# Own scores stored in one transfer, a weight load moved up, and a table tile read in six transfers by ScalarE's queue

## The chip, the cores and the metric

The kernel runs on one core of a Trainium2 chip. Its metric is the device time of one execution in microseconds (us). The engines are PE (TensorE, matrix products), DVE (VectorE), ACT (ScalarE), POOL (GpSimd) and SP (SyncE). Each has an instruction queue of its own that runs in order; they wait for each other by semaphores. ACT, POOL and SP also issue transfers (DMAs), which run beside the engines on 16 DMA engines. In the profile, q0 is POOL's queue of transfers, q1 SP's and q10 ACT's.

## The reference

The kernel computes two layers of a graph network on 625 nodes with 1024 features and 10000 edges. The changed part lies in the first layer, which adds to x a graph attention over the edges, a linear attention over all nodes and, after them, a small ternary feed-forward net. The graph attention is the part that matters here:

```python
xl = (x @ Wl).reshape(n, H, D)          # H = 4 heads of D = 64
xr = (x @ Wr).reshape(n, H, D)
msg = xl[src] + xr[dst]                 # per edge, and per node with itself
act = jnp.where(msg > 0, msg, NEG_SLOPE * msg)
e = jnp.einsum('ehd,hd->eh', act, att)
m = jax.ops.segment_max(e, dst, num_segments=n)
p = jnp.exp(e - m[dst])
denom = jax.ops.segment_sum(p, dst, num_segments=n)
alpha = p / (denom[dst] + 1e-16)
out = jax.ops.segment_sum(alpha[..., None] * xl[src], dst, num_segments=n)
```

An edge from each node to itself is added to the 10000. The linear attention computes keys, values and queries with 1024x1024 weights: `kv = sum over nodes of phi(k) v`, and the answer is `phi(q) kv / (phi(q) . sum phi(k))`, with `phi(x) = elu(x) + 1`. The second layer has a mean over neighbours in place of the graph attention, and a mixture of eight experts at its end; it takes most of the time and isn't touched.

## The kernel before, in words

The nodes are worked in NT = 5 tiles of P = 125. The edges are worked in 79 chunks of 128, two chunks to a group, 40 groups. The order of the work on each engine is the order in which the program records it; nothing reorders it afterwards.

**Scores of the edges.** Tile by tile PE makes xl and xr (`left_right`, `plr`), ACT copies them into `xlr` and stores xl to DRAM as `xl_d`, POOL stores xr as `xr_d`. A "beat" (`one_beat`) handles one group. POOL gathers, for each chunk, the rows of the source nodes (`ga`, from xl_d) and of the target nodes (`gb`, from xr_d), both at L601. DVE adds and scores them four and more beats later (`score_group`, L609 and after), ACT takes the exponential (`raise_all`, `es`, L588), and POOL scatters the four scores of each edge into `table`, a 625 by 625 table of four scores in DRAM (`scatter`, L619). POOL's order within a beat is gather, scatter, gather, scatter, ... All writes of the table are ordered: a scatter waits until the write of the table before it has landed. The table was filled with zeros by SP at the start (L395). So POOL's queue holds 79 gathers of each sort and 79 scatters.

**Own scores.** In beats 5 to 9 `self_loops(t)` scores each node of tile t with itself (`own`), and ACT stores these four scores onto the table's diagonal by `rows_dma` (L654), which makes two transfers, one of 112 rows and one of 13. These stores are writes of the table too: ACT waits for the scatter before them to land, and the next scatter on POOL waits for them.

**What runs beside it.** The linear attention is worked in two halves c of 512 features. `lin.half(1)` issues the second half's loads on SP: the biases `bk_t` and `bv_t`, then Wk and Wv, each as two transfers of 1 MB (`Half`). They use a ring of six weight buffers (`wpool`). The first half's Wk and Wv are loaded at the start, with `wd` and `wlr` in the other two buffers. `work(us)` is called as PE's work is recorded, and places the beats between its pieces. The calls of `lin.key(t)` and `lin.value(t)` for each tile are in the loops over c and t at L697 and after. Behind them come queries, answers and the output product (`mixed`, L733), during which the remaining beats run with shorter lags.

**From the table to the sums.** When the last scatter is issued, `load_table(t)` brings the table's rows of tile t into SBUF as `tb` (125 partitions, five slices of 125 by 4), by two transfers of 1093.8 and 127.0 KB on POOL's queue. `weigh(t)` multiplies them by the numbers of edges `CT`, in five DVE instructions, one for each slice (L828, `pT`); `sums(t)` lets PE add them up (`pg`); `turn_sums` and `up_again` bring the result into x. The order of POOL's transfers is tb(0), x(0), tb(1), x(1) to x(4), where x(t) is the tile of the input that the layer adds to (L1021). Further tiles of the table follow later.

Of the kernel before, what the change touches and what calls it, by code (L numbers as in the profile page):

```python
# [20 lines left out]
NT = 5  # L21
P = 125
# [20 lines left out]
def gps_kernel(tc: tile.TileContext, w: dict, out: bass.AP):  # L43

    again = attempt(tc, w, out, False)
    with tc.If(again > 0):
        attempt(tc, w, out, True)  # L50
# [3 lines left out]
def attempt(ctx: ExitStack, tc: tile.TileContext, w: dict, out: bass.AP, shifted: bool):  # L54

    nc = tc.nc
# [85 lines left out]
    def nodes(t):  # L142
        return slice(t * P, (t + 1) * P)
# [18 lines left out]
    def rows_dma(eng, dst, src):  # L162

        eng.dma_start(out=dst[0:112], in_=src[0:112])
        eng.dma_start(out=dst[112:P], in_=src[112:P])
# [32 lines left out]
    wpool = graph.enter_context(tc.tile_pool(name="w", bufs=6))  # L198
# [9 lines left out]
    hold = {}  # L208

    def mid(shape, name):  # L210
        return midp.tile(shape, FP, tag="mid", name=name)
# [135 lines left out]
    with ExitStack() as st0:  # L347
# [5 lines left out]
        tview = table[0:N * N, :].rearrange("(u p d) h -> p u (d h)", u=NT, p=P)  # L353
        xnT = bigT("xnT")

        with ExitStack() as edges:
# [22 lines left out]
            def load_edges():  # L379
                for dst, name in ((si, "src"), (di, "dst")):  # L380
# [10 lines left out]
            lin = LinearAttention(xnT, ("L0_Wq", "L0_Wk", "L0_bk", "L0_Wv", "L0_bv"), w["L0_bq"],  # L391
                                  lambda us: work(us), nc.sync)
# [3 lines left out]
                              in_=none.unsqueeze(1).to_broadcast([128, 28, 440]))  # L396
# [177 lines left out]
            def score(dst, m, n, p):  # L574

                by_att = att[0:p].unsqueeze(1).to_broadcast([p, n, 256])
                if shifted:
                    nc.vector.scalar_tensor_tensor(m, m, 0.2, m, op0=ALU.mult, op1=ALU.max)
                    nc.vector.tensor_tensor(m, m, by_att, op=ALU.mult)
                else:  # L580
                    nc.vector.scalar_tensor_tensor(m, m, 0.0, by_att, op0=ALU.max, op1=ALU.mult)
                nc.vector.tensor_reduce(dst, m.rearrange("p t (h e) -> p t h e", h=4), AX.X, ALU.add)
                if not shifted:
                    nc.vector.tensor_scalar(dst, dst, LIMIT, None, op0=ALU.min)

            def exp(e):
                if not shifted:
                    nc.scalar.activation(e, e, AF.Exp)  # L588
# [35 lines left out]
            own = pool.tile([P, NT, 4], FP, name="own")  # L624
# [8 lines left out]
            diagonal = table[0:N * (N + 1), :].rearrange("(s d) h -> s d h", d=N + 1)[:, 0, :]  # L633

            def self_loops(t):


                m = pool.tile([P, 1, 256], FP, tag="xd", name="gs", bufs=1)
                nc.vector.tensor_tensor(m[:, 0, :], xlr[:, t, 0:256], xlr[:, t, 256:512], op=ALU.add)
                score(own[:, t:t + 1, :], m, 1, P)  # L640
                exp(own[:, t:t + 1, :])
                rows = xlr[:, t, 0:256].rearrange("p (h e) -> p h e", h=4)
                if shifted:
                    nc.vector.tensor_copy(xl1[:, t, :, 0:64], rows)
                else:
                    nc.vector.tensor_tensor(m[:, 0, :], xlr[:, t, 0:256], att[:P], op=ALU.mult)
                    nc.vector.tensor_reduce(linear[:, t, :], m.rearrange("p t (h e) -> p (t h) e", h=4), AX.X, ALU.add)
                    part4 = pool.tile([P, 4, 1], FP, tag="part4", name="part4", bufs=2)
                    nc.vector.tensor_scalar(part4[:, :, 0], linear[:, t, :], -4.0 * LINEAR, 4.0 * LINEAR,
                                            op0=ALU.max, op1=ALU.min)  # L650
                    nc.scalar.activation(xl1[:, t, :, 64:65], part4, AF.Exp, scale=0.25)
                    nc.vector.tensor_tensor(xl1[:, t, :, 0:64], rows,
                                            xl1[:, t, :, 64:65].to_broadcast([P, 4, 64]), op=ALU.mult)
                rows_dma(nc.scalar, diagonal[nodes(t), :], own[:, t, :])  # L654

# [14 lines left out]
            def one_beat():  # L672
                g = beat["g"]
                beat["g"] += 1
                if 5 <= g < NT + 5:
                    self_loops(g - 5)
                if lags[1] > lags[0]:
                    raise_all(g - lags[1])
                    scores(g - lags[0])
                else:  # L680
                    scores(g - lags[0])
                    raise_all(g - lags[1])
                for j in range(G):
                    if g < len(groups):
                        gather(g, j, 0)
                        scatter(g - lags[2] - 1)
                        gather(g, j, 1)
                    scatter(g - lags[2])

            def work(us):  # L690
                beat["us"] += us

                while beat["us"] >= 2.0 + 5.2 * min(beat["g"], 6) + 8.1 * max(beat["g"] - 6, 0) and chunks:
                    one_beat()
# [2 lines left out]
            states = []  # L697
            for c in range(2):
                if c:
                    lin.half(c)  # L700
                for t in range(NT):
                    for f in (lin.key, lin.value):
                        f(t)
                        part["held"] = max(part["held"] - 1, 0)
                        for _ in range(6):
                            if count():
                                work(0.7)
                states.append(lin.states())
                if c == 0:
                    for f in states[0]:  # L710
                        f()
# [63 lines left out]
            for m in range(KC):  # L775
# [5 lines left out]
                if m < 3:  # L781
# [3 lines left out]
                                      in_=w[("w_gate", "w_up", "w_down")[m]].rearrange("(k p) n -> p k n", p=128))  # L785
# [28 lines left out]
        def load_table(t):  # L814

            hold["tb", t] = mid([P, NT, P, 4], "tb")
            if not shifted:
                rows_dma(nc.gpsimd, hold["tb", t].rearrange("p s d h -> p s (d h)"),
                         tview[:, :, t * 4 * P:(t + 1) * 4 * P])

        def weigh(t):

# [194 lines left out]


        load_table(0)
        for t in range(NT):  # L1020
            rows_dma(nc.gpsimd, x[:, t, :], xrows[t])  # L1021
            if t == 0:
                load_table(1)
# [9 lines left out]
        for p in range(NT + 2):  # L1033
# [29 lines left out]
            if p + 2 < NT:  # L1063
                load_table(p + 2)
# [187 lines left out]
    for b in range(NB_MIN, NB):  # L1252
        nc.gpsimd.dma_start(out=y_d[b * 128:(b + 1) * 128, :].rearrange("p (a n) -> p a n", a=4),
                            in_=zero.unsqueeze(1).to_broadcast([128, 4, 256]))
# [452 lines left out]
    for i in range(3):  # L1707
        d = 1 << i
# [240 lines left out]
```

## Time and profile before

| | us |
|---|---|
| median of 4 runs | 2201.38 |
| the four runs | 2202.71, 2202.16, 2194.34, 2200.61 |
| the profiled execution | 2203.11 |
| its span | 2201.3 |
| PE busy | 2110.1 (96%) |
| DVE, POOL, ACT busy | 712.4, 340.3, 194.0 |
| first gather on POOL | 57.72 |
| last scatter on POOL | 413.77 |
| end of the weighing of tile 0 | 429.46 |
| mean clock of PE, share of full speed | 0.980 |

In the rows of a timeline, the first number is the start in us from the start of the span, the second the time busy; then come the engine ("ACTq" and the like for the issue of a transfer by that engine), the line, the operation, the tiles (out<-in) with the number of instructions put together, and in square brackets how long the engine had been idle and what ended the wait. A row of waits gives the engine and tile that waited, what it waited for, the us in total, the number of times and the longest. A row of a window gives the stretch and, for PE, PE's weight loads, DVE, ACT and POOL, the time busy and the number of instructions; then PE's granted clock, the share of the DMA engines that was busy and GB/s. "PEclk" in the page has a digit for each fortieth of the span, in tenths of full speed, 9 for 90% or more.

### The profile page before, as it was taken

To read this page: it belongs to the slowest core of one execution; us is meant where nothing else is said; L and a number is where in the kernel's file an instruction comes from. 1 tells how busy PE (TensorE), PEld (TensorE's weight loads), DVE (VectorE), ACT (ScalarE), POOL (GpSimd) and SP (SyncE) were. 2 spreads that over 40 slices of the span, in tenths; PEclk is the share of its full clock that TensorE was granted. 3 is DMA by queue.
4 is the path that set the end of the run, shared out by engine and by line. 5 is a ranking of instruction groups with operands and counts; after the bars stand their busy time and mean duration, and the time that the engine had idled before them with its cause. 6 is when DMAs were issued, how large, how long until landed. Compare 5 with 4: busy or idle time off the path is not lost. (4 is left out here: it accounts for less than half of the span.)

```text
span 2201.3 us, 17365 instructions
## 1 busy us (share of the span) xinstructions
PE 2110.1 (96%) x6934; PEld 1211.7 (55%) x6934; DVE 712.4 (32%) x1214; ACT 194.0 (9%) x354; POOL 340.3 (15%) x349
## 2 busy tenths in 40 slices
PE   7999999589899999999999999999999999999998
PEld 6665564355455777754446777457744444444443
DVE  5786486467432740000122143322111111111012
ACT  2010110002201100000000111100000000000000
POOL 1676767400000200210000000110000000000011
PEclk9999999679999999999999999999999999999999
DMA  9235432440122110150303101022099988997732
GB/s 301 80 94 187 136 120 87 100 127 22 38 86 77 48 39 16 71 182 0 96 19 106 51 26 39 29 95 96 25 363 343 330 294 306 331 330 284 276 140 91
DMA packets 145848, 301.62 MB, mean 137 GB/s; under 512 B 12370, under 2 KB 22436, under 8 KB 145754
## 3 DMA queue, kind: packets, MB, share of 16 engines
q1 hardware_dynamic: 123700, 244.23, 31.2%
q0 software_dynamic: 17376, 46.42, 7.1%
q10 hardware_dynamic: 4678, 9.72, 1.4%
q8 instruction: 58, 0.95, 0.2%
q14 instruction: 36, 0.29, 0.0%
HBM read 277.49 MB, written 22.84 MB: 136 GB/s over the span
## 5 line engine op out<-in xcount | busy, mean ns | idle before, releaser
L130 PE MATMUL pu<-w,xgT 128*128 128x512 f32 x768 | 333.9, 593 | 1.9 <-DVE xgT L1243 1.9
L130 PEld LDWEIGHTS pu<-w,xgT 128*128 128x128 f32 x768 | 144.3, 190 | 174.6 <-issue 171.7
L130 PE MATMUL pyb<-w,hb 128*128 128x512 f32 x384 | 174.3, 599 | 2.4 <-ACT yb L105 2.1
L130 PE MATMUL pk<-w,xnT 128*125 128x512 f32 x320 | 141.4, 595 | 1.2 <-DMA w<-in_L_Wk_dram 1.0
L130 PE MATMUL pv<-w,xnT 128*125 128x512 f32 x320 | 141.8, 597 | 0.2
L130 PE MATMUL pq<-xnT,w 128*128 128x313 f32 x512 | 138.2, 429 | 1.0 <-DVE v L277 0.8
L130 PE MATMUL p<-tT,w 128*128 128x313 f32 x512 | 136.3, 428 | 0.4 <-DVE tT L1243 0.4
L130 PEld LDWEIGHTS pyb<-w,hb 128*128 128x128 f32 x384 | 70.0, 190 | 90.8 <-issue 74.7
L130 PEld LDWEIGHTS pq<-xnT,w 128*128 128x128 f32 x512 | 97.5, 191 | 40.0 <-DVE v L277 1.6
L1783 DVE TENSOR_TENSOR su<-pu,su 128x512 f32<-128x512 f32 x24 | 16.6, 691 | 314.6 <-ACT su L1782 314.6
L130 PEld LDWEIGHTS p<-tT,w 128*128 128x128 f32 x512 | 97.0, 190 | 37.7 <-issue 1.2
L130 PEld LDWEIGHTS pv<-w,xnT 128*125 128x125 f32 x320 | 60.1, 190 | 73.5 <-issue 72.0
L130 PEld LDWEIGHTS pk<-w,xnT 128*125 128x125 f32 x320 | 59.9, 190 | 73.3 <-issue 71.2
L619 POOL DMA_INDIRECT table<-es,at x79 | 84.3, 1067 | 64.2 <-issue 25.6
L1766 POOL DMA_INDIRECT xg<-rows_d,slots x12 | 11.4, 947 | 524.7 <-PE pxg L1773 449.0
L601 POOL DMA_INDIRECT gb<-xr_d,di x79 | 81.2, 1028 | 24.1 <-issue 23.5
L601 POOL DMA_INDIRECT ga<-xl_d,si x79 | 79.3, 1004 | 33.8 <-issue 29.4
L733 PE MATMUL px<-w,oT 128*125 128x512 f32 x160 | 71.9, 607 | 7.2 <-DVE kept L739 5.9
L1132 DVE TENSOR_TENSOR z<-pz,z 125x512 fp32r<-125x512 f32 x10 | 6.9, 692 | 196.8 <-ACT z L1130 196.8
L130 PE MATMUL px<-w,hT 128*125 128x512 f32 x160 | 70.3, 592 | 0.0
L130 PE MATMUL px<-w,oT 128*125 128x512 f32 x160 | 70.3, 592 | 0.0
L130 PE MATMUL ph<-meanT,w 128*128 128x313 f32 x256 | 70.1, 426 | 0.0
(366 smaller groups left out, 2523.8 us busy)
## 6 DMA issues: line engine op xcount, KB each, us to landing
w<-in_eW_dram SPq DMA_DIRECT2D x144, 1024.0 KB
w<-in_L_Wk_dram SPq DMA_DIRECT2D x8, 1024.0 KB
w<-in_L_Wv_dram SPq DMA_DIRECT2D x8, 1024.0 KB
w<-in_L_Wq_dram SPq DMA_DIRECT2D x8, 1024.0 KB
w<-in_L_Wo_dram SPq DMA_DIRECT2D x8, 1024.0 KB
w<-in_W_self_dram SPq DMA_DIRECT2D x8, 1024.0 KB
w<-in_W_neigh_dram SPq DMA_DIRECT2D x8, 1024.0 KB
w<-in_sW_dram SPq DMA_DIRECT2D x8, 1024.0 KB
```

The costliest lines, as they stand in the source:

```text
L130: nc.tensor.matmul(dst, lhsT=lhsT, rhs=rhs, start=(i == 0), stop=(i == len(pairs) - 1))
L601: nc.gpsimd.indirect_dma_start(out=ab[g][side][0:p, j, :], out_offset=None, in_=src[:, :], in_offset=bass.IndirectOffsetOnAxis(ap=ix[0:p, ...
L619: nc.gpsimd.indirect_dma_start(out=table[:, :], out_offset=bass.IndirectOffsetOnAxis(ap=at[0:p, lo + j:lo + j + 1], axis=0), in_=es[0:p, l ...
L733: nc.tensor.matmul(hold["px", t][:P, c, :], lhsT=oT[:, k, nodes(t)], rhs=wo[c](k), start=(k == 0), stop=(k == KC - 1 and keep is not None))
L1132: nc.vector.tensor_tensor(low, src, high.bitcast(FP), op=ALU.subtract)
L1766: nc.gpsimd.indirect_dma_start(out=xg, out_offset=None, in_=rows_d[:, :], in_offset=bass.IndirectOffsetOnAxis(ap=slots[:, b:b + 1], axis=0))
L1783: nc.vector.tensor_tensor(su, pu[:, 0, :], su, op=ALU.mult)
```

## The change

Three edits in the first layer:

1. `self_loops` no longer stores the own scores of each tile; at the last tile it stores those of all five tiles by two transfers, of 112x5x4 and 13x5x4 numbers.
2. The second half's Wk is loaded while the first half is worked: its two transfers are issued on SP at c == 0, t == 1, behind the first half's Wv. At the start of the second half only biases and Wv are loaded.
3. `load_table(0)` issues six transfers on ACT's queue, the 13 last rows of all slices first, then 112 rows of each of the five slices; it no longer issues any on POOL's. The other tiles of the table are read as before.

```diff
-                rows_dma(nc.scalar, diagonal[nodes(t), :], own[:, t, :])
+                if t == NT - 1:
+                    by_tile = diagonal.rearrange("(t p) h -> p t h", p=P)
+                    rows_dma(nc.scalar, by_tile, own)
...
             for c in range(2):
                 if c:
-                    lin.half(c)
+                    lin.biases(c)
+                    lin.wk, lin.wv = wk1, Half(wpool, w["L0_Wv"], c)
+                    lin.half(c, loaded=True, biased=True)
                 for t in range(NT):
+                    if c == 0 and t == 1:
+                        wk1 = Half(wpool, w["L0_Wk"], 1)
                     for f in (lin.key, lin.value):
...
             if not shifted:
-                rows_dma(nc.gpsimd, hold["tb", t].rearrange("p s d h -> p s (d h)"),
-                         tview[:, :, t * 4 * P:(t + 1) * 4 * P])
+                dst, src = hold["tb", t].rearrange("p s d h -> p s (d h)"), tview[:, :, t * 4 * P:(t + 1) * 4 * P]
+                if t == 0:
+                    nc.scalar.dma_start(out=dst[112:P], in_=src[112:P])
+                    for s in range(NT):
+                        nc.scalar.dma_start(out=dst[0:112, s, :], in_=src[0:112, s, :])
+                else:
+                    rows_dma(nc.gpsimd, dst, src)
```

The order of PE's and DVE's instructions stays the same. ACT's queue has eight issues fewer in the beats and six more after the last scatter. On POOL's queue the two issues of tb(0) are gone, and x(0) stands ahead of tb(1), right behind the last scatter.

## The prediction

> **What bounds the kernel now.** The page comes first: PE is busy nearly everywhere, and at full clock.
>
> ```profile
> PE 2110.1 (96%) x6934; PEld 1211.7 (55%) x6934; DVE 712.4 (32%) x1214; ACT 194.0 (9%) x354; POOL 340.3 (15%) x349
> PEclk9999999679999999999999999999999999999999
> PE py L130 3%; DVE x L1844 0%
> ```
>
> PE is at 96%. The clock falls in slices 8 and 9 (385 to 495 us), the end of the graph stage that the change edits. The chain that ended last reaches back only 3% and says nothing of it, so next come PE's and POOL's waits between 50 and 430 us.
>
> ```profile
> PE pg L130 <- DVE pT L828: 24.6, 5, 23.5
> PE pct L458 <- DVE ring L437: 4.5, 1, 4.5
> PE pk L130 <- DMA w<-in_L_Wk_dram: 1.0, 1, 1.0
> ...
> POOL table L619 <- DMA table<-es,at: 23.6, 13, 3.5
> POOL table L619 <- DMA table<-own: 6.4, 3, 3.0
> ```
>
> PE's one large wait is 23.5 us for pT. The timelines of POOL, DVE and PE show where it comes from.
>
> ```profile
> 103.39 1.02 POOL L619 DMA_INDIRECT table<-es,at  x1 [3.02 <-DMA table<-own]
> 112.45 1.04 POOL L619 DMA_INDIRECT table<-es,at  x1 [1.72 <-DMA table<-own]
> 121.96 1.06 POOL L619 DMA_INDIRECT table<-es,at  x1 [1.62 <-DMA table<-own]
> 166.30 1.02 POOL L619 DMA_INDIRECT table<-es,at  x1 [3.58 <-issue]
> 172.92 0.98 POOL L619 DMA_INDIRECT table<-es,at  x1 [3.08 <-DMA table<-es,at]
> 413.77 0.85 POOL L619 DMA_INDIRECT table<-es,at  x1 [1.92 <-DMA table<-es,at]
> 416.37 0.90 POOL L164 DMA_DIRECT2D tb<-table  x1 [1.76 <-DMA table<-es,at]
> ...
> 382.62 0.69 DVE L609 TENSOR_TENSOR ga<-ga,gb 128x512 f32<-128x512 f32 x1 [8.53 <-DMA gb<-xr_d,di]
> 424.62 4.84 DVE L828 TENSOR_TENSOR pT<-tb,CT 125x500 f32<-125x500 f32 x5 [23.88 <-DMA tb<-table]
> ...
> 425.71 0.68 PE L130 MATMUL pg<-xl,pT 125*125 125x65 f32 x2 [23.52 <-DVE pT L828]
> ```
>
> From 57.72 to 416.37 POOL issues its 237 gathers and scatters back to back, each about 1.0 us plus 0.3 of issue; a longer gap is a scatter waiting until the write before it has landed in the table. The scores are ready early (group 9's exponential ends at 147.65, its scatter starts at 178.96). At 382.62 DVE itself waits 8.53 us for gathers. So POOL's queue is the bound: what it gains carries over to 416, up to the 8.53 us at which DVE's own work would bind. Then come the table's tile tb(0), DVE's weighing, and PE. What PE or ACT gain earlier is swallowed by PE's waits near 385 and at 402.2.
>
> **The change part by part.** The profiled execution took 2203.11 us (span 2201.3 and 1.8 around it), 0.08% over the median of 2201.38; the sum is made against it and then scaled.
>
> *Key weights early.* SP issues two loads of 2.1 MB together right behind Wv0, once PE's last plr (45.24) and ACT's copy (45.97) free the slots. The DMA engines then move 395 GB/s (48 to 52), 264 (52 to 56) and 38 (56 to 60). The last piece of xl_d, issued by ACT at 52.55 because it waits for the table's fill, gates the first gather, and nothing else does: it took 4.9 us or so to land as the queues emptied; the like pieces of 13 KB that POOL stored in the full stretch took 5.3 to 6.2. So the gather moves by +0.4 to +1.3; I take the middle, +0.9. The floor is 0; the ceiling is the whole load going first, 2.1/0.39 = +5.4. What else is behind it: SP's next issue is bk_t at 146.25, far away; the next gathers land later, but a score is used five beats (40 us) on.
>
> What it takes from 158 on: Wk1, Wv1, Wq and one raw tile make 8.4 MB there (374 GB/s between 160 and 185). The five scatters at 166.30, 172.92, 178.96, 184.38 and 188.52 idle 3.58+3.08+2.47+1.52+0.55 = 11.2, 9.7 over the usual 0.30. (The third is put down to an exponential long done; it is the landing too.) With a quarter of the bytes gone, a quarter goes: −2.4. Ends: 0, if the remaining loads crowd the same scatters, and −5.4, all of the load's time. Wv1 and Wq wait for PE to free their slots, so they don't simply all move up. PE's 0.96 for Wk1 also goes, but is swallowed at 402.
>
> *Own scores once.* Eight of ten ACT issues go. ACT no longer stands at 89.8 to 99.07 and 100.3 to 109.43 for a scatter's landing; DVE's wait for kf (6.95 at 111.66) and PE's 4.54 at 112.98 shrink, ahead of the bound: 0. On POOL three scatters idle for own stores, 3.02+1.72+1.62 = 6.36, 5.46 over the usual; one such wait remains, as the last one (1.62, 1.32 over). It has five rows of 16 bytes for each partition rather than one: its growth lies between 0 and the 4.7 by which tb(0)'s 560 pieces (7.9 from issue) outlast the small store (3.23, from ACT at 118.73 to the scatter at 121.96). The bytes are few, as in the small store, so I take +0.7. −5.46 + 1.32 + 0.7 = **−3.4**. The exponential of tile 4 and the scores behind it on ACT now queue behind this one wait alone.
>
> *tb(0) in six on ACT's queue.* On POOL two issues (0.90 and 0.66) go; x(0) moves ahead, to about 414.9, then tb(1) after the last scatter's landing, then x(1) to x(4). ACT has nothing to do from 389.3 to 438.19, so nothing queues behind its wait. It woke 1.20 us after a scatter's end (117.53 to 118.73); the last ends at 414.62, so its first piece goes at 415.8 and its sixth 1.6 us later (0.31 each). DVE weighs slice by slice, 0.97 each, now with a wait for each piece. Before, weighing ended at 424.62+4.84 = 429.46. Lowest: the first slices land as fast as the small store (3.23) plus a fifth of the time for 1.22 MB, and DVE never waits again: 415.8+3.23+0.9+4.84 = 424.8, −4.7. Highest by sharing: where both queues ran together (1535 to 1538) POOL's queue moved 270 GB/s and SP's 133 of 401. At 133 the 1.22 MB takes 9.2: 415.8+3.23+9.2+0.97 = 429.2, −0.3. x(0) and tb(1) do run beside it now, but only 1.7 MB of them start in that time: midway, **−2.5**.
>
> Here a rule speaks against the edit: the Trainium skill, "DMA: Bandwidth & Descriptors", section "Issuing engines are not separate DMA queues", holds that transfers started by different engines share the same 16 DMA engines and that spreading them saves only issue time. By it the gain would be ACT's earlier waking alone, 416.37−415.8 = 0.6, and the sum 1.9 smaller. The two queues at 1535 agree about the sharing.
>
> What is late next: PE's pg group, 6.98 us at half clock behind pT, then a chain of turns between PE, DVE and ACT, unchanged. PE's idle time stays near 20 us, so the half clock from 407 to 444.8 stays.
>
> *Sum.* +0.9 − 2.4 − 3.4 − 2.5 = **−7.4**. POOL's part, −4.9, is under the cap of 8.53. 2203.11 − 7.4 = 2195.7; times 2201.38/2203.11 it is **2194.0**.
>
> **The rivals.**
>
> *B, larger.* tb(0) comes uncontended (−4.7 for −2.5), and the half-clock stretch at 475.5 to 496 falls away:
>
> ```profile
> 475.50:496.00 20.50, 15.21 (x63) 12.83 (x63) 11.27 (x25) 1.54 (x4) 2.00 (x3) 0.50 0.12 32
> ```
>
> PE was 15.21 busy there at 0.50, so without it some 5.5 would go (after PE's idles of 3.43 and 4.05 just before). For it: x tiles and tb(1) come earlier. Against: those idles come from DVE's and ACT's turns, not from DMA. With tb(0) alone −9.6, 2191.8; with both −15, 2186.
>
> *C, much of it eaten.* The burst's remaining loads crowd the scatters as before (0 for −2.4), and tb(0) crawls beside x(0) and tb(1) (−0.3 for −2.5): −2.8, 2198.6. For it: scatter stalls come in all later loads too (3.46 at 277.67, 2.83 at 339.13), and tb(1) took 12.3 us beside x. The case that the early load does nothing is in it.
>
> *D, the other side: tb(0) starved on ACT's queue.* POOL's queue holds x(0) to x(4) (2.56 MB) and tb(1) (1.22); if those were served first, at 270 GB/s from 414.7, they end at 428.7, and tb(0), landing 7.9 after that, as it did alone, has its last slice weighed at 437.6: +8.1 for −2.5, in all +3.2, 2206.3, or 2204.6 by the median. It decides from the point where weighing ends after 429.46+4.9 = 434.4. For it: the 270 to 133 at 1535. Against: 133 is no standstill, and x(2) waited for tb's landing before it was issued (2.67 at 424.18).
>
> **How the numbers follow.** The forecast as worked out holds 0.47 (2190 to 2198.5 by itself), B 0.15, C 0.25, D 0.13. About 0.3%, 6.6 us, is what a measurement tells from no change, so the border lies at 2194.8, inside the forecast. Faster: 0.31 of the forecast's 0.47, and B: 0.46. Slower by over 2208: part of D, with the start's ceiling of +5.4 and an added half-clock stretch, 0.12. Same: the rest, 0.42. The range drops B's second half and the worst of D: 2187 to 2205.
>
> **What would show it.** First gather near 58.6. One scatter stall for own, some 2 us, at about 121, where there were three. Four or five stalls from 160 to 190 that add up to about 8.8, and loads there of Wv1, Wq and raw only. Last scatter at about 408.9, and weighing ending near 422. DVE's wait at 382 shorter by some 5. Should the last scatter stand at 414 still, POOL's queue was not the bound, or the stalls reappeared further on; should weighing end more than 15.7 after that scatter's start, as before, the six transfers gave nothing. A half-clock stretch added or gone is worth 5 us, and would make the total wrong without a step being wrong.

## The result and the profile after

The changed kernel takes 2203.30 us (median of 34 runs), the kernel before 2200.32 in the same comparison (55 runs): ratio 1.0013, 95% interval 1.0007 to 1.0019. It is 0.13% slower, some 2.9 us. That lies inside the range on record, but the forecast of 2194.0 was a gain and this is a loss.

The profiled execution took 2202.27 us, span 2200.5, so it lies 1 us under its own median, as the one of before lay 2.8 over its. Single executions differ by a few us; stages are compared in the traces, the whole in the ratios. Lines of the timelines of POOL, ACT, DVE and PE of the changed kernel:

```profile
56.34 1.02 POOL L601 DMA_INDIRECT ga<-xl_d,si  x1 [8.37 <-issue]
117.33 0.98 POOL L619 DMA_INDIRECT table<-es,at  x1 [2.48 <-DMA table<-own]
160.78 0.98 POOL L619 DMA_INDIRECT table<-es,at  x1 [3.77 <-issue]
166.40 0.98 POOL L619 DMA_INDIRECT table<-es,at  x1 [2.12 <-DMA table<-es,at]
172.42 0.98 POOL L619 DMA_INDIRECT table<-es,at  x1 [2.52 <-DMA table<-es,at]
176.70 0.99 POOL L619 DMA_INDIRECT table<-es,at  x1 [0.30 <-issue]
...
408.20 0.85 POOL L619 DMA_INDIRECT table<-es,at  x1 [1.91 <-DMA table<-es,at]
409.05 0.59 POOL L164 DMA_DIRECT2D x<-in_x_dram  x1
410.70 0.86 POOL L164 DMA_DIRECT2D tb<-table  x1 [0.50 <-issue]
...
410.15 0.31 ACTq L826 DMA_DIRECT2D tb<-table  x1
410.50 2.43 ACTq L828 DMA_DIRECT2D tb<-table  x5
...
417.33 1.04 DVE L839 TENSOR_TENSOR pT<-tb,CT 125x500 f32<-125x500 f32 x1 [22.16 <-DMA tb<-table]
420.53 1.04 DVE L839 TENSOR_TENSOR pT<-tb,CT 125x500 f32<-125x500 f32 x1 [2.16 <-DMA tb<-table]
423.54 1.04 DVE L839 TENSOR_TENSOR pT<-tb,CT 125x500 f32<-125x500 f32 x1 [1.97 <-DMA tb<-table]
426.10 1.04 DVE L839 TENSOR_TENSOR pT<-tb,CT 125x500 f32<-125x500 f32 x1 [1.52 <-DMA tb<-table]
429.12 1.04 DVE L839 TENSOR_TENSOR pT<-tb,CT 125x500 f32<-125x500 f32 x1 [1.97 <-DMA tb<-table]
...
430.21 6.99 PE L130 MATMUL pg<-xl,pT 125*125 125x65 f32 x32 [2.32 <-DVE pT L839]
```

POOL's queue did what was forecast. One scatter waits for the own scores where three did, three scatters stall after 158 where five did, and the last scatter starts at 408.20 instead of 413.77, 5.57 us earlier (in these two executions; the start of the last scatter varies by some us, as batch f shows). Then it is all lost. The six pieces of tb(0) land some 3 us apart, DVE waits for each, and weighing ends at 430.16, 21.96 us after the last scatter's start. Before, it was 429.46 and 15.69. So the table's tile gives back 6.27 us, a little more than the queue had won, and PE's big group of pg starts 0.7 us later than before.

The windows show what the transfers moved meanwhile (the last two columns are the share of the DMA engines that was busy and GB/s), of the changed kernel, from 412 on; below them are its packets between 414 and 420, by queue (packets, MB, share of 16 engines):

```profile
412.00:416.00 4.00, 0.00 (x0) 0.00 (x0) 0.00 (x0) 0.00 (x0) 2.94 (x7) 0.50 1.07 161
416.00:420.00 4.00, 0.68 (x2) 0.50 (x2) 1.04 (x1) 0.00 (x0) 0.45 (x1) 0.50 1.02 272
...
DMA packets 440, 1.42 MB, mean 237 GB/s; under 512 B 35, under 2 KB 286, under 8 KB 440
q0 software_dynamic: 155, 0.92, 60.3%
q10 hardware_dynamic: 285, 0.50, 43.9%
```

The DMA engines are full, but only 0.50 MB of the 1.42 MB are tb(0), on ACT's queue q10; 0.92 MB are x(0), tb(1) and what follows on POOL's queue q0. That is 83 GB/s for tb(0), well under the 133 that the forecast took as its worst. q10's packets are under 2 KB (rows of 2000 bytes), q0's 154 larger ones about 6 KB each (0.92 MB/154). These six us are a mean of two unlike stretches, which are taken apart behind batch g.

### The profile page after: what moved, and what is told of

Same layout as the page of the kernel before. It is cut to its first block, busy times and chain, and to the rows that moved or that the text cites. A ratio compares the mean times of both kernels' runs of the same rounds, so it can differ in the third digit from the quotient of the medians.

```text
span 2200.5 us, 17358 instructions
## 1 busy us (share of the span) xinstructions
PE 2108.6 (96%) x6934; PEld 1212.3 (55%) x6934; DVE 713.3 (32%) x1214; ACT 193.9 (9%) x354; POOL 337.1 (15%) x347
## 5 line engine op out<-in xcount | busy, mean ns | idle before, releaser
L130 PEld LDWEIGHTS pq<-xnT,w 128*128 128x128 f32 x512 | 97.7, 192 | 40.3 <-DVE v L277 1.6
```

Source lines behind the costliest of these rows:

```text
L130: nc.tensor.matmul(dst, lhsT=lhsT, rhs=rhs, start=(i == 0), stop=(i == len(pairs) - 1))
```

## The experiments

Three theories were tried. *Theory 1*: edits 1 and 2 gain what POOL's queue shows, and the six transfers lose it, because POOL's transfers, which now run beside them, take the DMA engines from them. This could be because POOL's packets are larger (1a), or because POOL's queue goes first whatever its packets (1b). *Theory 2*: small pieces on ACT's queue are slow by themselves. *Theory 3*: what POOL's queue gains never reaches the end. The 15 runs came in four batches, e, f, g and h, each compared with the kernel before in the same batch. In e, g and h PE itself paused in the graph stage and every kernel took some 55 us longer, the kernel before 2256 us; so a ratio is read against the kernel before of its own batch.

**Batch e**, four kernels. e1_edits12: the changed kernel without edit 3.

```diff
-                if t == 0:
-                    nc.scalar.dma_start(out=dst[112:P], in_=src[112:P])
-                    for s in range(NT):
-                        nc.scalar.dma_start(out=dst[0:112, s, :], in_=src[0:112, s, :])
-                else:
-                    rows_dma(nc.gpsimd, dst, src)
+                rows_dma(nc.gpsimd, dst, src)
```

> The changed kernel with tile 0 of the table read by POOL's two transfers, as before; the own scores and the early key weights stay. Theory 1 (the six transfers on ACT's queue lose what POOL's queue gained, because POOL's larger packets take most of the DMA engines' time): last scatter at about 408.2 as in the changed kernel, weighing of tile 0 ends 15.7 us after its start, near 423.9, and the time is about 5.6 us under before, ratio near 0.9975. Rival theory 3 (what POOL's queue gains is lost further on whatever the table's transfer does, for example to a lower clock): weighing ends near 424 as well, but the ratio is 1.000 or more.

e2_six_only: the kernel before with this diff the other way round, that is, with edit 3 alone.

> The kernel before with the six transfers of tile 0 on ACT's queue alone. Theories 1 and 2 alike: the last scatter stays near 413.8, the weighing ends 22 us after its start as in the changed kernel, near 435.7, and the time is 6 us over before, ratio near 1.003. Theory 3: weighing the same, ratio not read from it.

e3_six_pool: the changed kernel with the six transfers on POOL's queue, ahead of x(0) and tb(1).

```diff
-                    nc.scalar.dma_start(out=dst[112:P], in_=src[112:P])
+                    nc.gpsimd.dma_start(out=dst[112:P], in_=src[112:P])
                     for s in range(NT):
-                        nc.scalar.dma_start(out=dst[0:112, s, :], in_=src[0:112, s, :])
+                        nc.gpsimd.dma_start(out=dst[0:112, s, :], in_=src[0:112, s, :])
```

> The changed kernel with the six transfers of tile 0 issued by POOL, ahead of x(0) and tb(1) in the same queue. Theory 1: nothing competes with them, the slices land about 1 us apart, limited by POOL's issues of 0.6 to 0.9 each, DVE weighs as they land, weighing ends some 12 us after the last scatter's start, near 420.5, and the time is 8 to 9 us under before, ratio near 0.996. Theory 2 (small pieces of 2000 bytes are slow by themselves, about 75 GB/s, on whichever queue): slices land 3 us apart again, weighing ends near 430, ratio near 1.000.

e4_held: the six stay on ACT's queue, but POOL first reads tb(0), and so waits for all of it, before it issues x(0) and the rest.

```diff
         load_table(0)
+        seen = late.tile([P, NT], FP, name="seen")
+        nc.gpsimd.tensor_copy(seen, hold["tb", 0][:, :, 0, 0])
         for t in range(NT):
             rows_dma(nc.gpsimd, x[:, t, :], xrows[t])
```

> The changed kernel, but POOL copies a few numbers of tile 0 of the table before it issues x(0), tb(1) and the rest, so that these start only when the six transfers on ACT's queue have landed. Theory 1: without company the 1.22 MB take 4 to 6 us, weighing ends between 416 and 419, and the time is 8 to 12 us under before unless the later loads are then late: ratio 0.995 to 0.997. Theory 2 (ACT's queue or its 2000 byte pieces are slow by themselves): slices still land 3 us apart, weighing ends near 430, POOL's loads start at 429 and the ratio is over 1.003.

Ratios: e1 1.0023 (1.0003 to 1.0043), e2 1.0040 (1.0023 to 1.0056), e3 1.0013 (0.9997 to 1.0030), e4 1.0016 (0.9998 to 1.0034). For the total this decides nothing between theories 1 and 3: e1's waits of PE and of POOL show that POOL's queue was not the bound.

```profile
PE pct L458 <- issue: 20.7, 25, 2.3
PE pkv L130 <- issue: 17.3, 1, 17.3
PE pv L130 <- issue: 12.9, 12, 2.5
...
POOL ga L601 <- DVE es L584: 47.2, 5, 14.3
```

PE waits for nothing that the profile shows, and POOL's gathers wait for DVE's scores (that these are late behind PE's work is a reading, not a row). But the stage after the last scatter can be read in any batch, and there the theories part. Weighing ends, counted from the last scatter's start: e1 15.8 us, e2 21.6, e3 11.7, e4 10.6.

**Batch f** repeats three of these kernels and adds one; here PE didn't pause (2199.96 before).

> The same kernel as e1_edits12, run again because on the first chip PE's own pauses of 0.7 us and multiples, some 60 us in the graph stage, set the pace and not POOL's queue (PE's wait for issue, 20.7 us at pct alone, and DVE's scores behind it). Where PE doesn't pause, theory 1: last scatter near 408, weighing ends near 424, ratio near 0.9975. Theory 3: weighing ends near 424 and the ratio is 1.000 or more. If PE pauses here too, the run says nothing of POOL's queue and the ratio should again lie between 1.000 and 1.004.

> The same kernel as e3_six_pool. Where PE doesn't pause, theory 1: weighing ends near 420.5, 12 us after the last scatter's start, and the ratio is near 0.996. Theory 3: weighing ends as early, ratio 1.000 or more.

> The same kernel as e4_held. Where PE doesn't pause, theory 1: weighing ends 8 to 11 us after the last scatter's start, between 416 and 419, ratio 0.995 to 0.997 unless x(0) or tb(1) come late for PE. Theory 2: weighing ends near 430, ratio over 1.003.

f5_own_only: the kernel before with edit 1 alone.

```diff
-                rows_dma(nc.scalar, diagonal[nodes(t), :], own[:, t, :])
+                if t == NT - 1:
+                    by_tile = diagonal.rearrange("(t p) h -> p t h", p=P)
+                    rows_dma(nc.scalar, by_tile, own)
```

> The kernel before with the own scores stored at once, and nothing else changed. Where PE doesn't pause: one scatter waits for own, 2.5 us, where three waited for 6.4; POOL's queue is 4 us ahead after it and ends at about 410, with weighing near 425.5: ratio near 0.998 by theory 1, 1.000 or more by theory 3.

| | ratio to before (95%) | last scatter | weighing ends | from the one to the other |
|---|---|---|---|---|
| before | | 413.77 | 429.46 | 15.7 |
| changed | 1.0013 (1.0007 to 1.0019) | 408.20 | 430.16 | 22.0 |
| f1, edits 1 and 2 | 0.9982 (0.9970 to 0.9995) | 412.43 | 428.18 | 15.8 |
| f3, six on POOL | 0.9972 (0.9960 to 0.9985) | 407.36 | 419.01 | 11.7 |
| f4, six on ACT, POOL held | 0.9992 (0.9982 to 1.0003) | 408.12 | 418.87 | 10.8 |
| f5, edit 1 alone | 0.9991 (0.9979 to 1.0002) | 409.14 | 424.60 | 15.5 |

f1 is faster: theory 3 falls, the queue's gain reaches the end. Edit 3 is what turns it: from 0.9982 to 1.0013, 0.31% or 6.8 us, against the 6.3 of the trace (the two ratios come from two comparisons; kernel before 2199.96 and 2200.32). f4 ends theory 2. With no company, DVE never waits after the first piece (its timeline, and the packets of f4 from 411 to 417):

```profile
414.03 4.84 DVE L839 TENSOR_TENSOR pT<-tb,CT 125x500 f32<-125x500 f32 x5 [18.97 <-DMA tb<-table]
...
DMA packets 716, 1.25 MB, mean 208 GB/s; under 512 B 93, under 2 KB 716, under 8 KB 716
q10 hardware_dynamic: 716, 1.25, 87.6%
```

All of tb(0) passes in under 6 us, in packets under 2 KB, on the same queue that brought 0.50 MB in 6 us in the changed kernel. f4's ratio isn't better than f1's for the reason that its expectation left open: x(0) and tb(1) are late now (f4's timelines of DVE and PE).

```profile
430.44 4.86 DVE L839 TENSOR_TENSOR pT<-tb,CT 125x500 f32<-125x500 f32 x5 [3.67 <-DMA tb<-table]
438.90 9.73 PE L739 MATMUL px<-w,oT 128*125 128x512 f32 x16 [4.26 <-DVE x L907]
```

PE's sums of tile 1 (the next `pg` group, of 40) start 40.3 us after the last scatter in f4, 39.0 in f1, 35.6 in f3, 39.9 before and 45.5 in the changed kernel. So f4 has given its head start back by then, and in the changed kernel the loss of the weighing is still there.

f3 has both: the pieces first and in order, and the rest right behind them in the same queue. It is the fastest kernel here, 2193.35 us, faster than before and than the changed one, though by 0.28% or 6.2 us where 8 to 9 were expected. Over f1 its 0.1% is inside the intervals. POOL issues the six in 3.3 us, and DVE's five instructions follow without a wait (f3's timelines):

```profile
409.99 0.68 POOL L826 DMA_DIRECT2D tb<-table  x1 [1.78 <-DMA table<-es,at]
410.66 2.65 POOL L828 DMA_DIRECT2D tb<-table  x5
414.18 4.83 DVE L839 TENSOR_TENSOR pT<-tb,CT 125x500 f32<-125x500 f32 x5 [19.84 <-DMA tb<-table]
426.83 4.84 DVE L839 TENSOR_TENSOR pT<-tb,CT 125x500 f32<-125x500 f32 x5
```

f1's own trace is a poor one for the queue: the same edits ended the scatters at 408.20, 407.36 and 408.12 in three other traces, and at 412.43 there. So the start of the last scatter varies by 4 to 5 us between executions of the same edits, and one trace doesn't price them; the ratios do.

**Batch g** was meant for the parts alone and for what sets the share of the two queues. g6_wk_only is the kernel before with edit 2 alone (its lines stand in the diff of the change), g2_six_only is e2 again.

> The kernel before with the second half's Wk loaded in the first half, and nothing else changed. Where PE doesn't pause: the first gather starts within 1.5 us of before; the scatter stalls between 150 and 190 add up to 8 to 9 us instead of 11; last scatter 2 to 4 us earlier. Theory 1: ratio 0.998 to 0.999. Theory 3: 1.000 or more.

> The same kernel as e2_six_only: before with the six transfers on ACT's queue alone. Where PE doesn't pause: slices 3 us apart, weighing ends 21 to 22 us after the last scatter's start, where before it ended 15.7 after it, ratio near 1.003.

g7_tb1_slices: in the changed kernel POOL reads tile 1 in slices too.

```diff
+                elif t == 1:
+                    nc.gpsimd.dma_start(out=dst[112:P], in_=src[112:P])
+                    for s in range(NT):
+                        nc.gpsimd.dma_start(out=dst[0:112, s, :], in_=src[0:112, s, :])
```

> The changed kernel, but POOL reads tile 1 of the table slice by slice too, so that its packets are 2000 bytes, as those of tile 0 on ACT's queue, and not 4000 and 6000. Theory 1a (the DMA engines take a packet from each queue in turn, so the queue with the larger packets gets the larger share): slices of tile 0 land about 1.8 us apart where both tiles are read, weighing ends 17 to 19 us after the last scatter's start, ratio about 0.001 under the changed kernel's 1.0013. Theory 1b (POOL's queue goes first whatever its packets): slices 3 us apart as before and weighing ends 22 after it.

g8_two_act: in the changed kernel tile 0 is read by ACT's queue in two transfers.

```diff
+                eng = nc.scalar if t == 0 else nc.gpsimd
+                rows_dma(eng, hold["tb", t].rearrange("p s d h -> p s (d h)"),
+                         tview[:, :, t * 4 * P:(t + 1) * 4 * P])
```

> The changed kernel with tile 0 of the table read by ACT's queue in two transfers, of 112 and 13 rows, as POOL read it before. If ACT's packets are 2000 bytes here too (theory 1a says so of the share), all of tile 0 lands as late as the last slice did, 20 us after the last scatter, and the five DVE instructions follow in one piece: weighing ends 25 us after the last scatter's start, ratio near 1.003. If the two transfers land 8 to 10 us after their issue, the split in six was what made it slow, and the ratio is under 0.999.

PE paused again, so g6 (1.0025, 1.0006 to 1.0043) and the others' ratios (g2 1.0031, 1.0010 to 1.0052; g7 1.0052, 1.0033 to 1.0071; g8 1.0048, 1.0025 to 1.0071) don't price the parts where POOL's queue is the bound. From the last scatter to the end of weighing: g2 21.2 us, the third time for edit 3; g7 18.6; g8 19.3.

g7 came out at theory 1a's time, with DVE's second and third slice 1.6 and 1.7 us after the one before. But its premise failed in part: of its packets between 474 and 480, 75 are still over 2 KB, and ACT's queue, all of whose 716 packets in f4 are under 2 KB, is not where they would be.

```profile
DMA packets 541, 1.18 MB, mean 196 GB/s; under 512 B 90, under 2 KB 466, under 8 KB 541
q10 hardware_dynamic: 412, 0.72, 70.1%
q0 software_dynamic: 129, 0.46, 35.5%
```

So reading tb(1) in slices does shift the share to tb(0), 0.72 MB against 0.46, but doesn't bring all of POOL's packets under 2 KB: x(1), in rows of 4 KB, is on that queue as well, and in f3, between 412 and 414, 68 of the 127 packets of POOL's queue are over 2 KB though it reads tb(0) in slices.

g8 missed its 25 us: two transfers on ACT's queue do less badly than six. Its packets show why there is a tail at all (478 to 484, then 484 to 489):

```profile
q10 hardware_dynamic: 553, 1.10, 72.1%
q0 software_dynamic: 154, 0.52, 28.5%
...
q0 software_dynamic: 228, 1.16, 89.8%
q10 hardware_dynamic: 101, 0.15, 13.4%
```

1.10 of the 1.25 MB get through in six us, with x(0) beside them; the last 0.15 MB take five more while POOL's queue has nine tenths of the engines' time, and all five DVE instructions wait for that rest.

What sets the share shows when the stretch is taken apart: the changed kernel from 412 to 416 and from 420 to 424, then f4 from 412 to 416, then e2 from 476 to 480.

```profile
q10 hardware_dynamic: 244, 0.44, 79.6%
q0 software_dynamic: 69, 0.21, 27.8%
...
q0 software_dynamic: 185, 0.64, 67.9%
q10 hardware_dynamic: 185, 0.32, 36.0%
...
q10 hardware_dynamic: 575, 1.02, 105.3%
...
q0 software_dynamic: 186, 0.63, 68.3%
q10 hardware_dynamic: 186, 0.32, 36.2%
```

Once both queues were in full flow they moved the same number of packets: 320 and 343 from 416 to 424 in the changed kernel, and in eight us of the repeats of edit 3 332 and 331 (e2, from 472), 340 and 333 (g2, from 481), 349 and 352 (h2, from 475). A packet of POOL's was larger, so tb(0) got 0.60 of 2.04 MB there, 75 GB/s. That is theory 1a; POOL's queue does not go first. It doesn't cover the whole stage: in g8's last five us it was 228 packets to 101.

The four us ahead of that are another matter. From 412 to 416 ACT's queue had most of the engines' time, 79.6%, and moved 0.44 MB, where f4 moved 1.02 in the same four us. Its packets took some 0.21 us of an engine each, in f4 0.12 (estimates: share times 16 engines times 4 us, by the packets). Six pieces alone don't do this (f4), and company alone doesn't either: beside POOL's packets from 420 to 424, ACT's took 0.12 us each again (36.0%). Why they were slow in those four us stays open. So by 416 tb(0) was 0.6 MB behind f4 from the slow packets, and what was left then went at POOL's larger packets' pace.

**Batch h**: the two parts once more, and the kernel before for its profile.

> Before with the six transfers on ACT's queue alone, a third time, for a chip on which PE doesn't pause. There the sum of parts asks for the difference between the changed kernel (1.0013) and f1_edits12 (0.9982): ratio 1.003, between 1.0015 and 1.0045, with weighing ending 21 to 22 us after the last scatter's start. If the six transfers cost nothing by themselves and lose only together with the other two edits, the ratio is 1.000. Where PE pauses, 1.003 to 1.004 as twice before.

> Before with the second half's Wk in the first half alone. Where PE doesn't pause: f1_edits12 (0.9982) less f5_own_only (0.9991) leaves 0.999 for it, with the scatter stalls from 150 to 190 adding up to 8 to 9 us instead of 11. If it is worth nothing, 1.000. Where PE pauses, 1.0025 as before.

> The kernel before, unchanged, for its profile on the chip of these runs. Where PE pauses, its waits for issue (pct, pv, pkv) and a clock near 0.967 stand in this trace too, about 50 to 70 us of them ahead of 480 us; where it doesn't, the trace is that of before, with three scatters waiting for own.

Here PE paused too: h2 1.0044 (1.0026 to 1.0062), weighing 21.0 us after the last scatter; h6 1.0002 (0.9983 to 1.0020). h0 shows the pauses in the unchanged kernel, where PE's pct and pv wait 19.6 and 10.6 us for nothing that the profile shows, POOL's gathers wait 51.5 us for DVE's scores, and weighing ended 16.0 us after the last scatter.

Edit 3 alone costs 0.40, 0.31 and 0.44% in the three batches, and 0.31% by difference where PE doesn't pause. Edit 2 alone has no ratio from a batch without pauses.

## Why the prediction was wrong, point by point

*What bounds the kernel.* Right as far as the runs go. f1 keeps only the two edits that shorten POOL's queue and is 0.18% faster; what these edits free on ACT and PE lies ahead of PE's long wait for pT, 25.5 us in f1. The cap of 8.53 us was misread, though. DVE's wait at 382 should have shrunk by 5 and stayed at 8.47 us (376.86). The group of scores ahead of it waits for its gathers too, 4.30 us at 371.75 before and 5.57 at 366.05 after, so the wait moved along with POOL's queue. It is the distance between two groups of gathers and no reserve of DVE's. How far away the cap is wasn't measured.

*The start.* Forecast +0.9, between +0.4 and +1.3; the first gather came 1.38 us earlier. It isn't the change: f5, which doesn't move Wk, starts at 56.27, f1, which does, at 57.74. What the early load costs there is less than the 1.4 us by which the start varies between executions.

*The burst.* Forecast −2.4. The stalls over the usual 0.30, summed over the scatters from 145 to 200, fell from 9.7 to 7.5 us, −2.2; they are 7.8 in f1, 8.7 in f3, 7.6 in f4 and 10.8 in f5, which doesn't move Wk. Part of it came back: from 260 to 380 the sum was 14.9 instead of 12.3, but 12.7, 10.3 and 11.6 in f1, f3 and f4, so no regular loss is shown.

*Own scores.* Forecast −3.4. Three waits of 6.36 became one of 2.48 (2.29, 2.21 and 2.50 in f1, f3 and f4; in f5 the wait there is 1.51 and put down to ACT's exponential): −3.3 with the usual 0.30 for the two that went. The growth of the one store was +0.9 for the +0.7 taken. The ratio of f5, −0.09%, is 2 us with an interval from −4.6 to +0.4.

*Their sum* was −4.9; f1 measured −0.18%, −4.0 us (−6.6 to −1.1). The profile of the changed kernel has −5.57 at the last scatter, and −4.2 if the start's luck is left out.

*tb(0) in six.* This is the step that failed. It was put at −2.5, "midway" between −4.7 and −0.3; measured +6.3 in the trace and +6.8 in the ratios. Two things in it were wrong. First, more than the 1.7 MB of x(0) and tb(1) ran beside it: x(1) to x(3) were issued by 415.9, before the third piece had landed, and between 411 and 429 POOL's queue moved 3.07 MB. Second, the upper bound of 133 GB/s was no bound: tb(0) got 83. It came from a stretch with other transfers, in which the engines moved 401 GB/s in all; here they moved 161 and then 272. The packets of that stretch, from 1535 to 1538 in the kernel before, already had the rule in them:

```profile
q0 software_dynamic: 213, 0.81, 67.8%
q1 hardware_dynamic: 203, 0.40, 35.9%
```

Nearly one packet for one, and 270 to 133 because POOL's were twice as large. With POOL's at 6 KB, as tb(1) has them here, the share had to be smaller. The forecast also had no term for the slow packets from 412 to 416.

ACT did wake early (410.15, 1.1 us after the last scatter's end; forecast 1.2) and issued in 0.3 to 0.5 us apiece where 0.31 was forecast, so the issue side of the step nearly held.

*Rival D* named the right place and the right sign, and came with the right threshold: weighing ends 22.0 us after the last scatter, above the 20.6 (434.4 − 413.77) from which it decides. Its mechanism, POOL's queue served first, is not what the packets show: from 416 on the queues took turns. Its price was +8.1 for a complete standstill; +6.3 was measured. It was given 0.13, by the arguments that 133 GB/s is no standstill and that x(2) had to wait for tb's landing before it was issued. That wait was an effect of tb(0) standing in the same queue, and the edit takes it away: in the changed kernel x(2) is issued at 413.26 without a wait. That was to be seen in the order of the queue.

*The rule* of the Trainium skill ("DMA: Bandwidth & Descriptors", "Issuing engines are not separate DMA queues") spoke against the edit and was right to. It allowed a gain of 0.6, and the runs show a loss: f4 and f3, in which nothing runs beside tb(0) from another queue, against the changed kernel. The page's section "Queues, rings and completion order" says that each engine takes turns between queues packet by packet; by that rule 6 KB against 2 KB would leave tb(0) 25% (an estimate). The trace agrees from 416 on: 26% between 416 and 420 (0.28 of 1.09 MB), and as many packets of the one queue as of the other. From 412 to 416, with 244 packets to 69, it doesn't show it.

*The same step done otherwise* gains what was hoped for. f3 ends the weighing 11.7 us after the last scatter, 4.0 earlier than before, near the −4.7 that was the step's best end; f4, with tb(0) alone on ACT's queue, ends it 4.9 earlier and loses that again behind it.

## What to carry to other kernels

A transfer that the critical path waits for doesn't get its own bandwidth by being put on another queue: what stood behind it now runs beside it. Keep it at the head of the queue that carries its competitors, split it there if its reader can work piece by piece, and let the rest follow. Ask of every transfer that an edit takes out of a queue what it had been holding back.

A sharing ratio from another stretch of the profile is no bound: ask how large the packets of each queue were there and will be here, and how much the engines moved in all.

## What the runs showed of the hardware that was not expected

Two queues in full flow shared by packets and not by bytes: 185 packets each between 420 and 424, 0.64 MB for POOL's and 0.32 for ACT's. And while the DMA engines were busy throughout, they moved 161 GB/s between 412 and 416 in the changed kernel, where ACT's queue alone moved 241 and 268 in the two halves of the same four us in f4; the cause stays open.

In three of four batches PE started single matmuls at distances of multiples of 0.7 us, with idle time between them, for some 20 us on end, in every kernel, the one before included. In h0 two such stretches are 75 to 92 and 162 to 187, with a granted clock of 0.61 and 0.54. Three rows of h0's timeline of PE:

```profile
87.00 0.42 PE L458 MATMUL pct<-ring 128*125 128x313 bf16 x1 [2.37 <-issue]
89.80 0.42 PE L458 MATMUL pct<-ring 128*125 128x313 bf16 x1 [2.38 <-issue]
91.20 0.42 PE L458 MATMUL pct<-ring 128*125 128x313 bf16 x1 [0.98 <-issue]
```

Starts are 2.80 and 1.40 us apart. The time before rises from 2200 to 2256 us and the bound in the graph stage goes from POOL's queue to PE. One chip had both kinds of batch (f and h), so it isn't the chip alone; what sets it off was not found, nor whether the low clock is its cause or its effect. In such a batch edits 1 and 2 together cost 0.23% (e1), which is not explained either.
